# Layer 0's masks added on TensorE for two sequences, and the late tiles' plan played in steps

## The chip, the cores and the metric

The kernel runs on one core of a Trainium2 chip. The metric is device time in microseconds (us) of one launch, as a median over runs.

## The reference

Four sequences of 256 tokens, 256 features wide (1024 tokens), pass through two layers. Each of the four blocks is preceded by a layer norm and followed by a residual addition.

1. Layer 0, attention: 16 heads of 16, q and k with rms-norm over 256 features and rope, a causal window of 128 keys:

```python
mask = (q_idx >= k_idx) & (q_idx - k_idx <= WINDOW - 1)      # WINDOW = 128
scores = jnp.einsum('bhqd,bhkd->bhqk', q, k) * scale
scores = jnp.where(mask[None, None], scores, -jnp.inf)
probs = jax.nn.softmax(scores, axis=-1)
```

2. Layer 0, feed-forward: 256 to 1024 to 256 with relu, weights stored as 4-bit integers with scales per block of 64, plus low-rank (rank 16) additions.
3. Layer 1, scan: `dt = softplus(...)`, `h[t] = exp(dt A) h[t-1] + dt B x` for 16 states per feature, `y = sum_n h C`.
4. Layer 1, a transformer block of its own: causal attention with 32 heads of 128 over 4 key heads, then a mixture of 32 experts (sigmoid router plus bias, 8 experts per token, their weights normalised) and a shared expert:

```python
_, idx = jax.lax.top_k(router_scores + expert_bias[None, :], TOPK)   # TOPK = 8
w = jnp.take_along_axis(router_scores, idx, axis=1)
w = w / jnp.sum(w, axis=-1, keepdims=True)
moe = jnp.einsum('tei,te,eih->th', act, wfull, Wd)                    # act = silu(g) * u
```

## The kernel before

**Streams and order.** The program is written as Python generators ("streams"). `timed(stream, (lo, hi, n), ...)` gives the parts of a stream (from one `yield` to the next) marks that run from `lo` to `hi`; `play` always continues the stream whose next mark is smallest, until those that must finish have done so. What is issued in that order lands on the queue of its engine in that order[...]. (SP only starts DMAs; scatters, DMAs with indices, are started by POOL.) PSUM is cut into banks of 128x512 f32: six of tag "w", which `ps(...)` hands out in turn, and two of tag "acc".

**Layer 0's attention**, `l0_attention(b)` for sequence b, has two tiles of 128 queries.
- `l0_project` makes q and k, normalised and rotated, in `qpads[t]` and `kpads[t]`: 32 columns per head, of which 16 are the features. `turn_heads` (L345, L346) transposes them, so that four heads lie at rows 0, 32, 64 and 96 of `qT` and `kT`. q carries a negative scale, so scores are negative of the usual ones, and the lowest stands for the largest.
- `l0_lowest`, once for each of eight pairs of heads, computes the scores of a head: queries of the first tile against 128 keys, queries of the second against 256, two matmuls with 16 rows each, into one bank `l0_sc` (L360). Then DVE runs two `tensor_tensor_reduce` per head (L367), each of which adds a mask (0 or a large number) and takes the minimum over the keys. The minimum goes to column 16 of the head in `qpads[t]`. In the profile each of them is a CUSTOM_DVE operation and a DVE_READ_ACCUMULATOR.
- `qpads` are then transposed anew (L345). With the constant −1 in column 16 of `kpads`, the 17-row products of `l0_softmax` (L381) give scores with the minimum taken off; ACT takes the exponential (L388), and POOL zeroes what the window excludes (L393, L397).
- `l0_values` (L409) multiplies by the values, `l0_divide` (L418 to L422) divides by the sum, `l0_close` (L430, L434) applies the output weights and adds to the residual x.

Sequence 0's attention is played together with the dequantisation of the feed-forward weights (L238, L241, L245, L250, with their low-rank products `lora_up` L240 and `lora_dn` L249) and the start of sequence 1. Sequence 1's `l0_lowest` then comes between parts of sequence 0's softmax, values, close and feed-forward (`feed_forward`, L460 to L503). Sequences 2 and 3 do layer 0 later, beside scans (L506 to L590) and layer 1's attention (L603 to L737) of earlier sequences.

**The experts.** `route(b)` computes the router for a sequence and, by prefix counts (`rank`), the place of every token and expert among the slots of that expert (`mo_at`, L909). POOL scatters the tokens' rows to these slots in DRAM: 16 scatters `slots<-mo_row,mo_at` a sequence (L918). Experts work on tiles of 128 slots; this input has 73 tiles with work. `plan(nm, n, early)` computes which expert each tile has and where its rows lie: an early plan, after the third sequence, for the first EARLY = 16 tiles, which are full already, and a late plan, after the last, for the others (LATE = 80 places). A plan is a chain of some 30 small DVE operations with two PE products in it: `late_pc` counts tokens per expert, `late_pv` (L831) spreads the result to all partitions. Out of `plan` come `regs` (first row and expert, loaded into registers), `which`, `lo`, `hi` and `arm`.

`experts` is pipelined over steps: load of a tile's rows (`slots_in`, L1215, on SP), transpose `flip` (L1225), gate and up products (`gate`, L1233), expert weight and destination `mx_wj`, `at` (`weigh`, L1248 to L1255), activation (L1263), transpose (L1268), down product (L1278), copy `mx_o` (L1286) and a scatter with addition to one of four sums in DRAM (L1287, on POOL). The first FEWEST = 64 steps are fixed; a Switch on the number of tiles chooses how many follow. At the end the four sums are read back and added to x (L1366, L1371).

The last route, the shared expert, the first 64 expert steps and the late plan are played together:

```python
def planned():
    yield
    tables.append(plan("late", LATE, False))
    yield
...
streams = [
    timed(shared(), (-1, 3, 2), (10, 18, 4)),
    timed(experts(FEWEST, range(FEWEST), under_way), (-2, FEWEST - 2, FEWEST)),
    timed(planned(), (6, 6, 2)),
]
play([timed(last_route[0], (0, 3, 3), (3, 5, 9))], streams)
```

Of the kernel before, what the change touches and what calls it, by code (L numbers as in the profile page):

```python
# [8 lines left out]
F32 = mybir.dt.float32  # L9
I32 = mybir.dt.int32  # L10
BF16 = mybir.dt.bfloat16
AF = mybir.ActivationFunctionType
ALU = mybir.AluOpType
AX = mybir.AxisListType
SYNC = mybir.DependencyInfo(mybir.DependencyClass.Sync, mybir.DependencyReason.DATA)

P = 128
# [8 lines left out]
NH0 = 16  # L26
HD0 = 16
# [16 lines left out]
EARLY = ((B - 1) * S * TOPK - NE * (P - 1)) // P  # L44
# [8 lines left out]
def block_kernel(ctx: ExitStack, tc, out, a):  # L53
    nc = tc.nc
    V, A, G, T = nc.vector, nc.scalar, nc.gpsimd, nc.tensor
# [3 lines left out]
    const = ctx.enter_context(tc.tile_pool(name="const", bufs=1, side="left"))  # L59
# [6 lines left out]
    def ps(name, tag="w"):  # L66

        return psum.tile([P, 512], F32, tag=tag, name=name, bufs=6 if tag == "w" else 2)
# [23 lines left out]
    early = ExitStack()  # L92
# [7 lines left out]
    ident = const.tile([P, P], F32, tag="ident", name="ident")  # L100
# [4 lines left out]
    masks = const.tile([P, 4 * P], F32, tag="masks", name="masks")  # L105
# [8 lines left out]
        pattern=[[1, P]], compare_op=ALU.is_gt, fill=BIG, base=0, channel_multiplier=-1,  # L114
    )
    mask_first = masks[:, P : 2 * P]
    mask_window = masks[:, 2 * P : 4 * P]
    mask_causal = masks[:, 0 : 2 * P]


    ones16 = const.tile([P, P], BF16, tag="ones16", name="ones16")
# [132 lines left out]
    l0 = early.enter_context(tc.tile_pool(name="l0", bufs=1, side="right"))  # L254
# [94 lines left out]
    def l0_pair(u):  # L349
        return [(2 * u + i, 32 * ((2 * u + i) % 4)) for i in range(2)], u // 2  # L350

    def l0_lowest(b, u, seq):

        pair, j = l0_pair(u)
        qT, kT = seq["qT"], seq["kT"]
        scs = [ps(f"l0_sc{b}_{h}") for h, _ in pair]
        for q, cols in ((0, slice(0, P)), (1, slice(P, 3 * P))):
            for (h, r0), sc in zip(pair, scs):
                rows_ = slice(r0, r0 + HD0)
                T.matmul(  # L360
                    sc[:, cols], qT[rows_, j, q * P : (q + 1) * P],
                    kT[rows_, j, 0 : cols.stop - cols.start], start=True, stop=True,
                )
        for (h, _), sc in zip(pair, scs):
            junk = l0.tile([P, 3 * P], F32, tag="junk", name=f"l0_junk{b}_{h}", bufs=1)
            for t, cols, mask in ((0, slice(0, P), mask_first), (1, slice(P, 3 * P), mask_window)):
                V.tensor_tensor_reduce(  # L367
                    junk[:, cols], sc[:, cols], mask, 1.0, 3.0e38,
                    ALU.add, ALU.min, seq["pads"][t][:, h, HD0 : HD0 + 1],
                )  # L370

    def l0_softmax(b, u, seq):

# [62 lines left out]
    def l0_attention(b):  # L436


        seq = {}
        yield from l0_project(b, seq)  # L440
        for u in range(NH0 // 2):
            l0_lowest(b, u, seq)
            yield
        for t in range(2):
            turn_heads(
                seq["qT"][:, :, t * P : (t + 1) * P], seq["pads"][t], f"l0_ptr{b}_{t}_2",
                V.tensor_copy if t == 0 else A.copy,
            )
        prs = {}
        for u in range(NH0 // 2 + 2):  # L450
            if u < NH0 // 2:
                prs[u] = l0_softmax(b, u, seq)
            if u >= 2:
                i = u - 2
                if i % 4 == 0:
                    seq["av"] = halves(ps(f"l0_av{b}_{i // 4}", "acc"))
                l0_values(b, i, seq, prs.pop(i))
                if i % 4 == 3:
                    l0_divide(b, i // 4, seq)
            yield  # L460
        l0_close(b, seq)
# [312 lines left out]
    def plan(nm, n, early):  # L774

        def small(name, n=NE, dtype=F32):
            return end[0].tile([P, n], dtype, tag=f"plan_{name}", name=f"{nm}_{name}", bufs=1)

        c16 = stat.tile([P, NE], BF16, tag="mo_chosen16", name=f"{nm}_c16", bufs=1)
        V.tensor_copy(c16, chosen)
        pc = ps(f"{nm}_pc")[:, 0:NE]

        T.matmul(pc, ones16, c16, start=True, stop=True)
        count, tiles, cum, junk = small("count"), small("tiles"), small("cum"), small("junk")
        ti = small("ti", dtype=I32)
        ex, one = small("ex", 1), small("one")
        total = small("total", 1)
        j, used, vals = small("j", 1), small("used", 1), small("vals", 3)  # L790
        V.tensor_copy(count, pc)
        V.tensor_scalar(ti, count, 0.0 if early else float(P - 1), None, ALU.add)
        V.tensor_scalar(ti, ti, 7, None, ALU.arith_shift_right)
        V.tensor_copy(tiles, ti)
        if not early:
            V.tensor_tensor(tiles, tiles, taken, ALU.subtract)
        V.tensor_tensor_scan(cum, ones_ne, tiles, 0.0, ALU.mult, ALU.add)
        V.tensor_copy(total, cum[:, NE - 1 :])
        V.tensor_scalar(junk, cum, part, None, ALU.is_le)
        V.tensor_reduce(ex, junk, AX.X, ALU.add)  # L800
        V.tensor_scalar(one, enum, ex, None, ALU.is_equal)
        V.tensor_tensor(cum, cum, tiles, ALU.subtract)
        if early:

            V.tensor_scalar(taken, cum, -1.0, float(EARLY), ALU.mult, ALU.add)
            V.tensor_scalar(taken, taken, 0.0, None, ALU.max)
            V.tensor_tensor(taken, taken, tiles, ALU.min)
        else:
            V.tensor_tensor(cum, cum, taken, ALU.subtract)

        V.tensor_tensor(junk, one, cum, ALU.mult)
        V.tensor_reduce(j, junk, AX.X, ALU.add)
        V.tensor_tensor(j, part, j, ALU.subtract)
        V.tensor_scalar(j, j, float(P), None, ALU.mult)
        if early:
            V.tensor_copy(vals[:, 1:2], ex)
            V.scalar_tensor_tensor(vals[:, 0:1], ex, float(CAP), j, ALU.mult, ALU.add)
        else:
            live = small("live", 1)
            V.tensor_tensor(junk, one, count, ALU.mult)  # L820
            V.tensor_reduce(used, junk, AX.X, ALU.add)
            V.tensor_scalar(live, ex, float(NE) - 0.5, None, ALU.is_lt)
            V.tensor_tensor(vals[:, 1:2], ex, live, ALU.mult)
            V.tensor_tensor(vals[:, 2:3], used, j, ALU.subtract)
            V.scalar_tensor_tensor(j, ex, float(CAP), j, ALU.mult, ALU.add)
            V.tensor_tensor(vals[:, 0:1], j, live, ALU.mult)

        rows_of = 2 if early else 3
        pv = ps(f"{nm}_pv")[:, 0 : rows_of * n].rearrange("p (q i) -> p q i", q=rows_of)
        for q in range(rows_of):  # L830
            T.matmul(  # L831
                pv[:, q, :], vals[:, q : q + 1].to_broadcast([P, P]), ident[:, 0:n],
                start=True, stop=True,
            )
        which = end[0].tile([P, n], F32, tag=f"{nm}_which", name=f"{nm}_which", bufs=1)
        V.tensor_copy(which, pv[:, 1, :])
        regs = end[0].tile([1, 2, n], I32, tag=f"{nm}_regs", name=f"{nm}_regs", bufs=1)
        V.tensor_copy(regs[:, 0, :], pv[0:1, 0, :])
        V.tensor_scalar(regs[:, 1, :], pv[0:1, 1, :], 2.0 * P, None, ALU.mult)
        if early:  # L840
            return regs, which, None, None, None

        arm = end[0].tile([1, 1], I32, tag="arm", name="arm", bufs=1)
        V.tensor_scalar(arm, total[0:1], float(EARLY - FEWEST), None, ALU.add)

        lo = end[0].tile([P, n], F32, tag="lo", name="lo", bufs=1)
        hi = end[0].tile([P, n], F32, tag="hi", name="hi", bufs=1)
        spare = small("spare", 1)
        V.tensor_scalar(spare, part, float(CAP), None, ALU.add)
        V.tensor_scalar(lo, pv[:, 2, :], part, spare, ALU.is_le, ALU.mult)  # L850
        V.tensor_scalar(hi, lo, float(CAP - 1), None, ALU.max)
        return regs, which, lo, hi, arm

    taken = stat.tile([P, NE], F32, tag="taken", name="taken", bufs=1)

    LATE = -(-(TILES - EARLY) // 4) * 4
# [3 lines left out]
    def route(b, row):  # L860
# [51 lines left out]
            )  # L912

        if b == B - 2:
            tables.append(plan("early", EARLY, True))
        for t in range(2):
            for k in range(TOPK):
                inst = G.indirect_dma_start(  # L918
# [58 lines left out]
    def timed(stream, *pieces):  # L977


        marks = [lo + (hi - lo) * i / n for lo, hi, n in pieces for i in range(n)]  # L980
        return [stream, marks, 0, False]
# [346 lines left out]
            yield  # L1328


    def planned():
        yield
        tables.append(plan("late", LATE, False))
        yield

    under_way = ahead, {}, {}, {}, {}, {}, {}, {}
    streams = [
        timed(shared(), (-1, 3, 2), (10, 18, 4)),
        timed(experts(FEWEST, range(FEWEST), under_way), (-2, FEWEST - 2, FEWEST)),
        timed(planned(), (6, 6, 2)),  # L1340
    ]
    play([timed(last_route[0], (0, 3, 3), (3, 5, 9))], streams)
    with tc.manual_schedule():
# [137 lines left out]
```

## Time and profile before

| | us |
|---|---|
| time before, median of 3 runs | 1109.64 |
| lowest and highest of these | 1108.83, 1111.13 |
| profiled execution, its own time | 1098.13 |
| profiled execution, span of its trace | 1096.4 |

| engine | busy, us | share of the span | instructions |
|---|---|---|---|
| PE (matmul) | 932.8 | 85% | 4589 |
| DVE | 727.3 | 66% | 2237 |
| POOL | 510.1 | 47% | 534 |
| ACT | 491.1 | 45% | 1503 |

The stages, by the start of their instructions in the trace of the profiled execution: sequence 0's projections to 32 us, its scores to 57.7, softmax, values and close to 106.3, its feed-forward to 138.0, its scan to 223.7, layer 1's attention for all sequences from there to 902, the last route to 914.4, the remaining scatters to 1074.6, and the final sums to the end.

Times in a trace are counted in us from the start of the span. PE is TensorE's matmul row and PEld its weight loads; DVE is VectorE, ACT ScalarE, POOL GpSimd. "L360" is line 360 of the kernel. The granted clock is the share of full speed at which TensorE ran; over the whole span it is 0.908 in the mean. A line of a timeline gives start, duration, engine, line, operation, output and inputs, count, and in brackets the idle time before it and what ended that. A line of a group gives count, busy time and mean duration in ns, and idle time before it.

### The profile page before, as it was taken

What the parts mean: (1) busy time and instruction counts of PE and PEld (TensorE: products, weight loads), DVE (VectorE), ACT (ScalarE), POOL (GpSimd) and SP (SyncE); (2) the same over time, 40 slices, a digit from 0 to 9 for tenths busy, and PEclk for the clock granted to TensorE, in tenths of its full rate; (3) what the DMA queues carried; (4) which work ended last, traced back from release to release, by engine and by line L of the source; (5) the groups of instructions that cost most, each with busy time, mean ns of one, the idle gap of its engine ahead of it and who ended that gap; (6) DMA issues with size and microseconds to landing.
All of it is one profiled execution on the core that took longest, in us unless ns stands there. A gap on an engine that the chain in (4) does not pass through costs nothing. (4 is left out here: it accounts for less than half of the span.)

```text
span 1096.4 us, 15761 instructions
## 1 busy us (share of the span) xinstructions
PE 932.8 (85%) x4589; PEld 696.5 (64%) x4589; DVE 727.3 (66%) x2237; ACT 491.1 (45%) x1503; POOL 510.1 (47%) x534
## 2 busy tenths in 40 slices
PE   4898976478898999999899989899998997999770
PEld 2655743355666687767677766677877875777650
DVE  6746149947996775899686489896475536555454
ACT  2031233324655364656555466655564554444330
POOL 5030123413456332344865135775335624888781
PEclk9576776788898999999999989999999998999995
DMA  8985999960110111111222473223223327799867
GB/s 214 236 180 132 255 246 241 245 217 26 39 49 30 39 39 38 49 49 49 62 80 71 134 226 101 72 99 101 68 83 99 108 84 252 147 155 150 155 73 206
DMA packets 131716, 134.31 MB, mean 123 GB/s; under 512 B 10592, under 2 KB 125440, under 8 KB 131616
## 3 DMA queue, kind: packets, MB, share of 16 engines
q1 hardware_dynamic: 118032, 114.12, 39.0%
q0 software_dynamic: 13584, 19.05, 9.6%
q8 instruction: 40, 0.66, 0.3%
q14 instruction: 60, 0.49, 0.1%
HBM read 70.45 MB, written 62.69 MB: 121 GB/s over the span
## 5 line engine op out<-in xcount | busy, mean ns | idle before, releaser
L607 POOL TENSOR_TENSOR at_q_rot<-at_q_t,at_q_t 128x512 f32<-128x512 f32 x64 | 85.0, 1328 | 139.6 <-DVE at_q_t L603 116.8
L686 ACT ACTIVATE at_pr<-at_pr,at_low 128x128 f32<-128x128 f32 (+1 forms) x256 | 113.6, 445 | 52.0 <-DVE at_low L682 49.7
L737 PE MATMUL at_po<-at_wo,at_oT 128*128 128x256 f32 x512 | 129.6, 387 | 2.2 <-ACT at_oT L730 2.1
L655 PE MATMUL at_pq<-at_hT,at_wq 128*128 128x256 f32 x512 | 125.7, 389 | 3.1 <-DVE at_q_t L603 1.8
L696 POOL TENSOR_SCALAR at_pr<-at_pr,at_rden 128x128 f32<-128x128 f32 x128 | 87.8, 695 | 80.4 <-DVE at_rden L691 62.9
L1287 POOL DMA_INDIRECT sum<-mx_o,at x73 | 113.8, 1559 | 24.1 <-issue 9.4
L581 POOL TENSOR_TENSOR sm_y<-sm_y,sm_hc 128x512 f32<-128x512 f32 x60 | 77.2, 1287 | 86.0 <-DVE sm_hc L579 82.9
L655 PEld LDWEIGHTS at_pq<-at_hT,at_wq 128*128 128x128 f32 x512 | 98.0, 196 | 19.7 <-DVE at_q_t L603 2.0
L737 PEld LDWEIGHTS at_po<-at_wo,at_oT 128*128 128x128 f32 x512 | 95.4, 193 | 17.3 <-ACT at_oT L730 3.4
L603 DVE TENSOR_TENSOR at_q_t<-at_pq,rope 64x512 f32<-64x512 f32 x128 | 88.1, 688 | 15.4 <-POOL at_k_rot L607 12.9
L568 ACT ACTIVATE decay<-sm_dt,na 128x255 f32<-128x255 f32 x128 | 58.7, 500 | 64.4 <-DVE sm_h L574 58.4
L574 DVE TENSOR_TENSOR_SCAN sm_h<-decay,sm_w 128x512 f32<-128x512 f32 x64 | 84.5, 1320 | 1.3
L719 ACT COPY at_pT<-at_pa 128x512 f32<-128x512 f32 x64 | 37.2, 581 | 104.1 <-PE at_pa L712 104.0
L918 POOL DMA_INDIRECT slots<-mo_row,mo_at x64 | 64.4, 1007 | 39.0 <-DVE mo_at L909 21.1
L682 DVE CUSTOM_DVE_ANT_0 at_pr<-at_sc,masks 128x128 f32<-128x128 f32 (+1 forms) x256 | 78.4, 353 | 4.6 <-PE at_sc L678 3.0
L678 PE MATMUL at_sc<-at_k_rot,at_q_rot 128*128 128x256 f32 x256 | 76.5, 380 | 0.0
L727 PE MATMUL at_pav<-at_pT,at_v 128*128 128x512 f32 x128 | 67.4, 609 | 2.8 <-DVE sm_hc L579 1.3
L601 DVE TENSOR_TENSOR at_q_t<-at_pq,rope 128x512 f32<-128x512 f32 x64 | 43.8, 684 | 38.4 <-PE at_pq L655 38.0
L393 POOL TENSOR_SCALAR_AFFINE_SELECT l_pr<-l_pr 128x512 f32<-128x512 f32 x32 | 22.4, 700 | 97.7 <-ACT l_pr L388 97.7
L700 ACT ACTIVATE at_pr<-at_pr,at_rden 128x256 f32<-128x256 f32 x128 | 57.9, 501 | 8.2 <-DVE at_rden L691 8.0
L677 PEld LDWEIGHTS at_sc<-at_k_rot,at_q_rot 128*128 128x128 f32 x256 | 47.9, 190 | 12.7 <-issue 2.7
L1233 PE MATMUL bank<-wgu,mx_xT 128*128 x192 | 52.0, 394 | 3.9 <-DVE mx_act L1263 3.4
(357 smaller groups left out, 2038.9 us busy)
## 6 DMA issues: line engine op xcount, KB each, us to landing
slots<-zero SPq DMA_DIRECT2D x32, 1156.0 KB, 20.3
at_wq<-in_Wq_dram SPq DMA_DIRECT2D x64, 256.0 KB, 2.7
at_wo<-in_Wo_dram SPq DMA_DIRECT2D x64, 256.0 KB, 2.8
xg<-slots SPq DMA_DIRECT2D x73, 144.5 KB, 3.1
sum<-zero SPq DMA_DIRECT2D x4, 1152.0 KB, 12.7
wgu<-in_Wg_dram SPq DMA_DIRECT2D x32, 128.0 KB, 3.0
wgu<-in_Wu_dram SPq DMA_DIRECT2D x32, 128.0 KB, 3.3
wd<-in_Wd_dram SPq DMA_DIRECT2D x8, 512.0 KB, 6.7
```

Of the source, the lines that this page charges most:

```text
L574: V.tensor_tensor_scan(hs.rearrange("p c l -> p (c l)"), da.rearrange("p c l -> p (c l)"), w.rearrange("p c l -> p (c l)"), 0.0, ALU.mult, ...
L581: G.tensor_tensor(y, y, hc, ALU.add)
L603: V.tensor_tensor(t2[lo : lo + 64], src[hi : hi + 64], sin[hi : hi + 64].unsqueeze(1).to_broadcast([64, n, S]), ALU.mult,)
L607: G.tensor_tensor(dst, t1, t2, ALU.add)
L655: T.matmul(pq[:, i, :], wq[:, c, i * HD : (i + 1) * HD], hT[:, c, :], start=c == 0, stop=c == 1,)
L678: T.matmul(sc[:, P : 3 * P], qT[:, i, P:S], kT[:, 0, :], start=True, stop=True)
L682: V.tensor_tensor_reduce(pr[:, cols], sc[:, cols], mask, 1.0, 3.0e38, ALU.add, ALU.min, low[:, k : k + 1],)
L686: A.activation(pr[:, cols], pr[:, cols], AF.Exp, scale=-1.0, bias=low[:, k : k + 1], accum_out=den[:, k : k + 1],)
L696: scaled.append(G.tensor_scalar(prs[i][:, cols], prs[i][:, cols], rden[:, k : k + 1], None, ALU.mult).ins)
L727: T.matmul(pav, v_sb[:, 0, cols], pT[0], start=True, stop=False)
L737: T.matmul(po[:, t, :], oT[:, i, t * P : (t + 1) * P], wo[:, i, :], start=h0 + i == 0 and t == 0, stop=h0 + i == NH - 1 and t == 1, skip_g ...
L1287: G.indirect_dma_start(out=sums[i % SUMS], out_offset=bass.IndirectOffsetOnAxis(ap=at, axis=0), in_=o, in_offset=None, compute_op=ALU.add,)
```

## The change

There are two parts.

First, in sequences 0 and 1 the masks reach the scores on TensorE. A bf16 identity and a bf16 copy of the three 128x128 mask blocks are made once. For each head a matmul of the two (128x128 by 128x384) starts the bank, and the two score matmuls accumulate onto it. One `tensor_reduce` per head then takes the three minima of 128 keys into a small tile `low`; once per sequence, `l0_lowered` brings them into column 16 of `qpads`: a copy for the first query tile, and the smaller of two for the second. Sequences 2 and 3 keep the former code as `l0_lowest_late`.

Second, `plan` becomes a generator that yields between its operations. The early plan is still run through at once. The late plan is a stream of its own with marks from 5 to 13 in 11 parts, in place of a single part at mark 6.

```diff
+    ident16 = const.tile([P, P], BF16, tag="ident16", name="ident16")
+    masks16 = const.tile([P, 3 * P], BF16, tag="masks16", name="masks16")
+    V.tensor_copy(ident16, ident)
+    V.tensor_copy(masks16, masks[:, P:])
...
     def l0_lowest(b, u, seq):
 
+        pair, j = l0_pair(u)
+        qT, kT = seq["qT"], seq["kT"]
+        scs = [ps(f"l0_sc{b}_{h}") for h, _ in pair]
+        for sc in scs:
+            T.matmul(
+                sc[:, 0 : 3 * P], ident16, masks16, start=True, stop=False, skip_group_check=True
+            )
+        for q, cols in ((0, slice(0, P)), (1, slice(P, 3 * P))):
+            for (h, r0), sc in zip(pair, scs):
+                rows_ = slice(r0, r0 + HD0)
+                T.matmul(
+                    sc[:, cols], qT[rows_, j, q * P : (q + 1) * P],
+                    kT[rows_, j, 0 : cols.stop - cols.start],
+                    start=False, stop=True, skip_group_check=True,
+                )
+        for (h, _), sc in zip(pair, scs):
+            V.tensor_reduce(
+                seq["low"][:, h, :], sc[:, 0 : 3 * P].rearrange("p (c k) -> p c k", c=3),
+                AX.X, ALU.min,
+            )
+
+    def l0_lowest_late(b, u, seq):
+
         pair, j = l0_pair(u)
...
+    def l0_lowered(seq):
+
+        low = seq["low"]
+        at = slice(HD0, HD0 + 1)
+        V.tensor_copy(seq["pads"][0][:, :, at], low[:, :, 0:1])
+        V.tensor_tensor(seq["pads"][1][:, :, at], low[:, :, 1:2], low[:, :, 2:3], ALU.min)
...
         yield from l0_project(b, seq)
+        seq["low"] = l0.tile([P, NH0, 3], F32, tag="low", name=f"l0_low{b}", bufs=2)
         for u in range(NH0 // 2):
-            l0_lowest(b, u, seq)
+            (l0_lowest if b < 2 else l0_lowest_late)(b, u, seq)
             yield
+        if b < 2:
+            l0_lowered(seq)
...
         T.matmul(pc, ones16, c16, start=True, stop=True)
+        yield
         count, tiles, cum, junk = small("count"), small("tiles"), small("cum"), small("junk")
...
-        return regs, which, lo, hi, arm
+        tables.append((regs, which, lo, hi, arm))
...
         if b == B - 2:
-            tables.append(plan("early", EARLY, True))
+            for _ in plan("early", EARLY, True):
+                pass
...
-    def planned():
-        yield
-        tables.append(plan("late", LATE, False))
-        yield
-
...
-        timed(planned(), (6, 6, 2)),
+        timed(plan("late", LATE, False), (5, 13, 11)),
```

The diff shows one of ten such `yield`s in `plan`. The order of instructions per engine, before and after, differs as follows. POOL's and SP's orders are the same. PE gets 32 loads of `ident16` and 32 mask matmuls; one `lora_up` product goes behind the first pair of scores; `late_pc` comes earlier, and `late_pv` some four expert steps later. On DVE, the four instructions per head (32 heads) become one, and four small ones are new; sequence 0's last two reductions come ahead of a `w_dn` addition that they stood behind; the late plan's operations lie between those of the expert steps; `late_c` goes ahead of the last route's `mo_at`, and `late_count` stands between its two `mo_at` operations.

More of the change, by code (lines that the diff above doesn't have):

```diff
@@ L116, in block_kernel @@
     mask_first = masks[:, P : 2 * P]
-    mask_window = masks[:, 2 * P : 4 * P]
     mask_causal = masks[:, 0 : 2 * P]
+    ident16 = const.tile([P, P], BF16, tag="ident16", name="ident16")
+    masks16 = const.tile([P, 3 * P], BF16, tag="masks16", name="masks16")
+    V.tensor_copy(ident16, ident)
+    V.tensor_copy(masks16, masks[:, P:])
     ones16 = const.tile([P, P], BF16, tag="ones16", name="ones16")
@@ L365, in l0_lowest @@
             junk = l0.tile([P, 3 * P], F32, tag="junk", name=f"l0_junk{b}_{h}", bufs=1)
-            for t, cols, mask in ((0, slice(0, P), mask_first), (1, slice(P, 3 * P), mask_window)):
+            for t, cols, mask in ((0, slice(0, P), mask_first), (1, slice(P, 3 * P), masks[:, 2 * P :])):
                 V.tensor_tensor_reduce(
@@ L796, in plan @@
             V.tensor_tensor(tiles, tiles, taken, ALU.subtract)
+        yield
         V.tensor_tensor_scan(cum, ones_ne, tiles, 0.0, ALU.mult, ALU.add)
         V.tensor_copy(total, cum[:, NE - 1 :])
+        yield
         V.tensor_scalar(junk, cum, part, None, ALU.is_le)
@@ L801, in plan @@
         V.tensor_scalar(one, enum, ex, None, ALU.is_equal)
+        yield
         V.tensor_tensor(cum, cum, tiles, ALU.subtract)
@@ L809, in plan @@
             V.tensor_tensor(cum, cum, taken, ALU.subtract)
+        yield
         V.tensor_tensor(junk, one, cum, ALU.mult)
@@ L814, in plan @@
         V.tensor_scalar(j, j, float(P), None, ALU.mult)
+        yield
         if early:
@@ L826, in plan @@
             V.tensor_tensor(vals[:, 0:1], j, live, ALU.mult)
+        yield
         rows_of = 2 if early else 3
@@ L834, in plan @@
             )
+        yield
         which = end[0].tile([P, n], F32, tag=f"{nm}_which", name=f"{nm}_which", bufs=1)
@@ L840, in plan @@
         if early:
-            return regs, which, None, None, None
+            tables.append((regs, which, None, None, None))
+            return
+        yield
         arm = end[0].tile([1, 1], I32, tag="arm", name="arm", bufs=1)
         V.tensor_scalar(arm, total[0:1], float(EARLY - FEWEST), None, ALU.add)
+        yield
         lo = end[0].tile([P, n], F32, tag="lo", name="lo", bufs=1)
```

## The prediction

> **What bounds the kernel now.** I read the slices of the page first, then a table of windows cut at the stage borders, then the chain, and last the timelines of the places that the change touches.
>
> ```profile
> PE   4898976478898999999899989899998997999770
> DVE  6746149947996775899686489896475536555454
> PEclk9576776788898999999999989999999998999995
> ```
>
> One slice is 27.4 us. PE is the full row nearly everywhere, and its clock is low only in the first eleven slices, where layer 0 runs. The windows (us, then busy time and count per engine, granted clock, DMA share, GB/s) give each stage its limit:
>
> ```profile
> 31.00:50.30 19.30, 18.01 (x79) 13.03 (x78) 14.97 (x60) 0.58 (x1) 0.00 (x0) 0.50 0.91 230
> 57.70:82.00 24.30, 23.56 (x130) 14.53 (x130) 9.32 (x25) 10.23 (x30) 8.73 (x16) 0.78 0.78 174
> 82.00:106.30 24.30, 22.68 (x111) 13.85 (x110) 15.47 (x53) 2.70 (x6) 2.51 (x4) 0.65 0.42 118
> 106.30:124.00 17.70, 14.07 (x43) 9.76 (x44) 5.76 (x28) 2.67 (x7) 1.26 (x1) 0.61 1.10 245
> 165.70:223.70 58.00, 27.11 (x97) 17.89 (x95) 54.37 (x73) 16.58 (x40) 22.36 (x18) 0.68 1.09 246
> 245.00:902.00 657.00, 611.82 (x3113) 469.38 (x3112) 478.16 (x1427) 363.20 (x1113) 318.73 (x344) 0.98 0.25 75
> 934.70:1074.60 139.90, 115.61 (x595) 92.18 (x592) 70.43 (x332) 52.44 (x195) 113.81 (x73) 0.95 0.82 133
> ```
>
> Sequence 0's scores (31 to 50) are PE-bound, 18.01 of 19.30 us, at half clock all the way; DVE is close behind. 82 to 106 is PE again, with sequence 1's scores between sequence 0's value products. Then sequence 0's feed-forward, its scan (DVE, 54.4 of 58 us), and from 245 layer 1's attention on PE. Each stage starts with the result of the one before, and the order within an engine is fixed at build time, so what sequence 0's chain loses in layer 0 shifts all that follows. The tail is another matter:
>
> ```profile
> DMA 7%; PE 3%; issue 2%; DVE 1%; POOL 1%; SPq 0%; ACT 0%; POOLq 0%; DVEq 0%
> 914.37 1.03 POOL L918 DMA_INDIRECT slots<-mo_row,mo_at  x1 [21.09 <-DVE mo_at L909]
> 934.70 1.62 POOL L1287 DMA_INDIRECT sum<-mx_o,at  x1 [0.31 <-DVE at L1253]
> ```
>
> The page's chain covers only the last seventh. POOL's timeline says more: from 914.37 it issues 16 scatters of slots at 1.265 us each, then at once 73 scatters of sums at 1.86 us, with no gap over 0.3 us except 1.8 us about the Switch. What starts POOL at 914.37 is mo_at of the last route; from there POOL sets the end.
>
> **The late plan in steps.** Before, its instructions stand as one block on DVE (914.7 to 922.7) and PE waits 4.66 us for late_vals ahead of late_pv (919.85). All lies under POOL's scatters. The first mx_o is ready at 928.75, 6 us before POOL reaches its scatter at 934.70, so the wait removed is worth 0. It issues no DMA; SP's loads of expert numbers and rows, POOL's queue and their order stay the same. What moves: late_c goes ahead of the route's mo_at; late_count, which waits for PE's late_pc, now stands between the two mo_at operations, with the second and its scatters behind it. The first is not behind it. POOL needs the second eight scatters later, 10 us, and late_pc waits at most one expert's products (some 2 us). If that cover were gone it would cost those 2 us. late_pv comes four expert steps later, and its values are first needed for steps from EARLY on: the 16 slots and 16 sum scatters, some 50 us, cover it. Between −0.3 and +0.3, I take 0.
>
> **DVE in the scores.** Groups by form, 30 to 58 (busy, mean ns of one | idle before):
>
> ```profile
> L360 PE MATMUL l_sc<-l_kT,l_qT 16*128 16x256 f32 x32 | 11.6, 643 | 0.0
> L360 PE MATMUL l_sc<-l_kT,l_qT 16*128 16x128 f32 x32 | 9.4, 486 | 1.3 <-DVE qpad L367 1.3
> L367 DVE CUSTOM_DVE_ANT_0 l_junk<-l_sc,masks 128x256 f32<-128x256 f32 x16 | 6.7, 420 | 0.0
> L367 DVE CUSTOM_DVE_ANT_0 l_junk<-l_sc,masks 128x128 f32<-128x128 f32 x16 | 4.6, 287 | 3.3 <-PE l_sc L360 2.2 <-DVE qpad L367 0.6
> L367 DVE DVE_READ_ACCUMULATOR2_ANT qpad<- 128x1 f32 x32 | 2.7, 84 | 0.0
> ```
>
> A head now takes two custom operations and two reads, 0.56 us from start to start (41.07 to 41.63 in DVE's timeline). One TENSOR_REDUCE over 384 columns replaces them. No row has that form; the custom pair gives 0.13 us more per 128 columns, so 0.42 + 0.13 = 0.55 us long, some 0.48 of pitch: a gain of 0.1 × 16 = 1.3 to 1.6 us a sequence. At the floor it is the 256-column custom's 0.34 of pitch (gain 3.5), at the ceiling 0.65 (loss 1.5). Since PE ends last, the gain counts only where PE waits on DVE for a bank. The two conversions to bf16 lie at 4 to 11 us, where DVE waits for loads and for POOL: 0, and 0.3 us each if that cover were gone. The two small operations of l0_lowered cost some 0.2 us each, and stand between the last reduction and the transposes; they are in the gain above. The change issues no DMA; SP's zero fills, which wait for sequence 0's dequantisation buffers (62.6 to 95), shift with that sequence and are done by 232, long before the first sum scatter.
>
> **The masks on PE.** 32 products 128x384 in bf16, each with the load of ident16. The nearest row is sel, at half clock and 256 columns, six in a row:
>
> ```profile
> 159.11 1.46 PE L561 MATMUL sm_pbc<-sm_bc,sel 96*128 96x256 bf16 x6
> 88.78 1.65 PE L360 MATMUL l_sc<-l_kT,l_qT 16*128 16x128 f32 x8
> 90.36 1.50 PE L409 MATMUL l_av<-l_pr,l_v 128*32 128x256 f32 x8
> 91.78 1.65 PE L360 MATMUL l_sc<-l_kT,l_qT 16*128 16x128 f32 x8
> 42.51 2.06 PE L360 MATMUL l_sc<-l_kT,l_qT 16*128 16x128 f32 x14
> ```
>
> Successive starts are 0.21 us apart, so 384 columns are 0.32 us at half clock and 0.16 at full. The Trainium skill ("TensorE: Matmul & The Clock Gate", Part 1) says that the clock is full after one busy window of about 3.4 us. The row 31.00:50.30 speaks against that: PE shows 18.01 of 19.30 us busy at 0.50. In this trace the clock rises only after 128-row products nearly fill such a stretch (L290 and L292 from 59.3: full at 64.8). By the rule the stage would be at full clock and a mask cost 0.16 (16 × 0.16 = 2.6); by the trace 0.32 (5.1). I take the trace.
>
> Second, the masks stand between pairs. Scores of 16 rows for different heads run beside each other: 14 matmuls start inside 42.51 to 44.1, some 0.55 us per head with neighbours following on, against 1.58 us per pair (0.79 per head) where other work stands around it, as at 88.78. The skill's "TensorEngine Tiling (Array Packing)", Key Properties, says a change of tiling mode drains TensorE, which speaks against this change: by it every pair becomes an isolated one, 8 × 0.48 = 3.8 us more. The trace shows several pairs already apart, by lora products or waits (16 matmuls take 4.34 us from 45.95). I take 1.5 and keep 0 and 3.8.
>
> Sequence 0: masks 16 × 0.32 = +5.1, overlap +1.5, waits of PE on DVE that a shorter DVE takes up −2.5 (1.3 in the groups' PE row; the loads' row has 2.5), and −0.9 at the end, where its last two reductions no longer stand behind w_dn (54.12, itself waiting 2.12 us for lora_dn). Sum +3.2. Its softmax, 57.72, starts near 61.
>
> Sequence 1: its pairs lie on sequence 0's path in 82 to 119. Twelve heads at half clock, four at full: 12 × 0.32 + 4 × 0.16 = +4.5. Overlap +0.8 (pairs at 82 to 84 only; those after are isolated already). Off that −1.7, for one clock window of 3.4 us that the masks' 128-row work keeps at full near 82. Sum +3.6.
>
> Total +6.8 on the span of 1096.4. The profiled execution itself took 1098.13, 11.5 under the median of 1109.64; the shift is the same to either, so 1109.6 + 6.8 = 1116.4.
>
> **Rivals.**
> 1. The clock stays up (faster). The masks are full-array work: 0.64 us of a 3.4 us window per pair. At 85.3 the clock falls and at 102.4 it rises. If it holds at 1.0 there, three pairs with their values shrink from 3 × 3.07 to 3 × (0.80 + 0.75 + 0.32) us, −3.6, and 97.5 to 102 by 2.2. With masks of pairs at full clock (+1.3), sequence 0's +3.2, and one window won before the rise at 122.9 (ff_pu from 113.5), −3.4, the sum is −4.7: 1104.9. It decides on one window, 82 to 85.3, now filled by scores that leave most of the array empty. For it: 75 to 82 is at full clock on similar mixed work. Against: 85 to 95 contains 128-row value products half the time and stays at 0.50. 0.25.
> 2. One of the two stretches only, or DVE's cover is larger than I read (11.1 of 12.3 us busy in 38 to 50): PE's additions go partly into waits. 0 ± 2: 1109.6. 0.17.
> 3. The steps don't do what they say: the Switch's number comes late, so POOL starves at step 16. Place: 950 or so; price: one plan's 8 us. Needs late_pv later by over 30 us. 0.03, time 1124.
>
> **How the numbers follow.** A measurement of this kernel can tell about 0.2% (2.2 us) from no change. The forecast (1112.5 to 1121) has 0.55, rival 1 0.25, rival 2 0.17, rival 3 0.03. Faster 0.25; same 0.15 (rival 2 but its edges); slower 0.60. The range 1105 to 1121 leaves out the better half of rival 1 and rival 3 with the worst overlap; the forecast's own range is 1112.5 to 1121.
>
> **What would show it.** Right: a mask group 128x384 near 0.32 us pitch in sequence 0; softmax of sequence 0 (57.72) at 60 to 62; x add L434 (106.27) at 112 to 114; the first slots scatter (914.37) near 921, and the same 160 us from it to the last sum scatter. Wrong: the clock at 0.78 or more in 82 to 106, or the shift at L434 below 3 us; or a gap in POOL's row after 914, which would make the plan the cause.

## The result: 0.5% slower, and the profile after

The changed kernel takes 1113.66 us in the median of 20 runs (1102.18 to 1116.01), the kernel before 1107.36 in 20 (1103.61 to 1111.13). The ratio is 1.0049 with an interval of 1.0033 to 1.0065: 5.4 us slower by the ratio, 6.3 by the medians. The prediction had +6.8.

Its profiled execution took 1109.11 us with a span of 1107.4; that of before had 1098.13 and 1096.4, less than the shortest of the 20 runs of before here (1103.61). The two spans differ by 11.0 us, more than the medians, so the pair must be read stage by stage. The slices of the page after:

```profile
PE   4999876378899999999999988899989995999770
DVE  6644249947995865899686489885575533655453
PEclk9585876788898999999999989999999996999895
```

The windows of the changed kernel, cut at the same borders (us, then busy time and count per engine, granted clock, DMA share, GB/s):

```profile
31.30:52.60 21.30, 21.30 (x91) 9.51 (x88) 14.70 (x27) 0.58 (x1) 0.00 (x0) 0.50 0.90 233
58.30:79.30 21.00, 20.29 (x128) 12.85 (x128) 9.59 (x25) 10.21 (x30) 8.10 (x15) 0.88 0.81 185
79.30:111.50 32.20, 31.50 (x124) 17.61 (x124) 13.83 (x16) 2.70 (x6) 2.58 (x6) 0.58 0.51 134
916.50:940.40 23.90, 10.22 (x40) 7.84 (x39) 6.96 (x44) 3.94 (x15) 15.41 (x16) 0.65 0.55 205
940.40:1081.20 140.80, 121.72 (x629) 99.85 (x627) 75.11 (x356) 53.91 (x201) 112.25 (x72) 0.95 0.82 132
```

In the first, PE is now busy for all of it, still at half clock. The second is shorter than before (21.0 against 23.5 us, at 0.88 instead of 0.78), the third longer (32.2 us, at 0.58; before, the same work went from 81.2 to 106.3). Then the tail: 24.0 us where the kernel before had 20.3, and 140.8 where it had 136.0. The groups of the score stage, 30 to 62:

```profile
L370 PE MATMUL l_sc<-l_kT,l_qT 16*128 16x256 f32 x32 | 8.5, 629 | 0.0
L376 DVE TENSOR_REDUCE l_low<-l_sc 128x3 f32<-128x384 f32 x16 | 8.3, 553 | 6.5 <-PE l_sc L370 6.5
L364 PE MATMUL l_sc<-masks,ident 128*128 128x384 bf16 x16 | 6.6, 515 | 0.0
L370 PE MATMUL l_sc<-l_kT,l_qT 16*128 16x128 f32 x32 | 6.4, 497 | 0.0
```

DVE now waits 6.5 us for PE's scores. The reduction takes 0.553 us, as estimated (0.55). Laid side by side, the two traces have these stages (us, from the first start named to the second):

```
                                                   before    after
first score -> softmax of sequence 0                25.69    26.97
softmax -> first denominator (l_den)                23.48    21.02
first denominator -> residual addition (x, l_po)    25.06    32.23
residual addition -> scan's first step              60.18    57.06
scan's first step -> attention of layer 1           71.18    71.17
attention of layer 1 -> first of the last slots    676.74   676.71
first of the last slots -> first sum scatter        20.33    23.98
first -> last sum scatter                          136.02   140.78
```

Only 2.8 us of the 11.0 are in front of layer 1's attention, and 8.4 in the tail, where the prediction had put 0. (The first score, or mask, itself starts 0.7 us earlier, so attention starts 2.1 us later.) So there were two theories, and a third on the clock:

- A: the prediction. The masks are paid on PE's path in both sequences; the plan costs nothing, and the tail of this one trace has another cause.
- B: the plan in steps lets POOL starve in the tail, and the masks cost little.
- C: what changes is mostly where the stretches at half clock fall.

The comparisons below were made on three chips, where the kernel before took 1098.82, 1100.23 and 1106.04 us; each ratio is to the kernel before on the same chip.

### The profile page after: what moved, and what is told of

Read it like the earlier page. It is cut to its first block, busy times and chain, and to the rows that moved or that the text cites. A ratio compares the mean times of both kernels' runs of the same rounds, so it can differ in the third digit from the quotient of the medians.

```text
span 1107.4 us, 15719 instructions
## 1 busy us (share of the span) xinstructions
PE 941.0 (85%) x4621; PEld 696.8 (63%) x4621; DVE 724.6 (65%) x2147; ACT 490.6 (44%) x1503; POOL 509.3 (46%) x534
## 4 chain that ended last, share of the span: by engine, by line
PE 49%; DVE 26%; POOL 6%; issue 5%; DMA 5%; ACT 5%; another core or an unknown queue 1%; SPq 1%; POOLq 0%; DVEq 0%; ACTq 0%
PE at_po L776 5%; PE at_pq L694 5%; DVE sm_h L613 4%; DVE at_q_t L642 4%; PE bank L1284 3%; PE at_pav L766 3%; PE ff_pu L521 3%; DMA sum<-mx_o,at 2%; PE l_sc L370 2%; PE l_sT L417 2%; DVE sm_hc L618 2%; PE at_sc L717 2%; DVE sm_w L611 2%; DVE at_pr L721 2%; PE ff_pd L536 2%
```

## The experiments

**Parts of the change, one at a time.** The plan in steps alone (former scores everywhere), the masks alone (plan as one block), and the masks in one sequence only:

```diff
-            (l0_lowest if b < 2 else l0_lowest_late)(b, u, seq)
+            l0_lowest_late(b, u, seq)                            # plan only
...
-        timed(plan("late", LATE, False), (5, 13, 11)),
+        timed(planned(), (6, 6, 2)),                             # masks only
...
-            (l0_lowest if b < 2 else l0_lowest_late)(b, u, seq)
+            (l0_lowest if b == 0 else l0_lowest_late)(b, u, seq) # one sequence; b == 1 likewise
```

> The late plan in steps, with the former scores in all four sequences. Theory A (the prediction): the plan is hidden under POOL's scatters, 0 +- 1 us against the kernel before, and 20.3 us from the first of the last 16 slots scatters to the first sum scatter. Theory B (the tail): the stall of the changed kernel's trace there (23.9 us, then five gaps in POOL's row, 10.5 - 2.1 = 8.4 us in all) comes from the plan's steps lying between the expert steps; then +5 to +9 us here, with gaps in POOL's row after the first sum scatter.

> Masks on TensorE in sequences 0 and 1, with the late plan as one block as before. Theory A: +5 to +8 us, all of it there when sequence 0's residual addition after the attention starts. Theory B: +1 to +3 us, since the changed kernel's trace shows layer 1's attention only 2.1 us later. Theory C (the clock's windows): the front's shift depends on how the half-clock stretches fall, between -2 and +6, and the 12 first layer-0 windows tell.

> Masks on TensorE in sequence 0 alone, plan as one block. Theory A: +3.2 (2 to 5), softmax of sequence 0 starts near 61. From the changed kernel's trace (58.29 against 57.72, the scores starting 0.7 earlier) it is rather +0.6 to +1.3 at that point; then the rest is the clock's.

> Masks on TensorE in sequence 1 alone, plan as one block. Theory A: +3.6 (2 to 6), seen between 81 and the residual addition of sequence 0. Theory C: sequence 0's output products (12 of l_po) fall in a half-clock window, 5.35 instead of 2.86 us, as in the changed kernel; +5 there, partly given back by 140.

Measured: plan only 1.0014 (0.9996 to 1.0032), masks only 1.0023 (1.0004 to 1.0041), masks in sequence 0 0.9996 (0.9979 to 1.0013), in sequence 1 1.0015 (0.9993 to 1.0038). Only masks-only is clear of 1, by a little; the traces say more. First score to softmax is 25.67 in plan-only and 25.31 in sequence-1-only, but 26.98 in masks-only and in sequence-0-only: masks in sequence 0 cost 1.3 to 1.7 us there. First denominator to residual addition is 28.17 and 28.23 where sequence 1 has no masks, 32.23 and 32.36 where it has: 4.1 us, with the output products l_po at half clock in all four. The clock alone moves this stretch nearly as much: with the former scores in sequence 1 it takes 25.06 us in the profile of before and 25.07 to 28.23 in four others. So of the 7.2 us between the first two profiles, some 3 are theory C's. From the first of the last slots scatters to the first sum scatter all four take 20.31 to 20.36, plan-only as well.

Where the 4.1 us of sequence 1 are is seen in PE's timeline, the first lines of plan-only, the next of masks-only, both at half clock:

```profile
86.71 1.50 PE L442 MATMUL l_av<-l_pr,l_v 128*32 128x256 f32 x8
88.13 1.65 PE L386 MATMUL l_sc<-l_kT,l_qT 16*128 16x128 f32 x8
89.72 1.50 PE L442 MATMUL l_av<-l_pr,l_v 128*32 128x256 f32 x8
...
98.34 2.18 PE L386 MATMUL l_sc<-l_kT,l_qT 16*128 16x128 f32 x8
100.45 5.49 PE L463 MATMUL l_po<-wo,l_oT 128*128 128x256 f32 x12
```

```profile
89.49 1.50 PE L445 MATMUL l_av<-l_pr,l_v 128*32 128x256 f32 x8
90.92 0.82 PE L364 MATMUL l_sc<-masks,ident 128*128 128x384 bf16 x2
91.67 1.65 PE L370 MATMUL l_sc<-l_kT,l_qT 16*128 16x128 f32 x8
93.25 1.50 PE L445 MATMUL l_av<-l_pr,l_v 128*32 128x256 f32 x8
...
102.38 0.53 PE L364 MATMUL l_sc<-masks,ident 128*128 128x384 bf16 x1
102.83 1.64 PE L370 MATMUL l_sc<-l_kT,l_qT 16*128 16x128 f32 x4
104.41 0.50 PE L364 MATMUL l_sc<-masks,ident 128*128 128x384 bf16 x1
104.84 1.65 PE L370 MATMUL l_sc<-l_kT,l_qT 16*128 16x128 f32 x4
106.42 5.48 PE L466 MATMUL l_po<-wo,l_oT 128*128 128x256 f32 x12
```

A pair with its values takes 3.76 us in place of 3.01: 0.75 for two masks. The last pair before l_po takes 4.04 instead of 2.11: there one head's mask stands between the two heads' scores, and the second head no longer runs beside the first.

**The changed kernel again.**

> The changed kernel once more, beside the kernel before on this chip, and with a second profile of it. If the wait of 8.4 us in the tail of its first profile belongs to the kernel (theory B), the second has it too, near 24 us from the first of the last slots scatters to the first sum scatter. If it was one execution's (theory A), 20.3 us as in the four kernels so far, and the time is the sum of masks and plan alone, +2 to +6.

Measured: 1.0039 (1.0016 to 1.0062), and 20.32 us from the first of the last slots scatters to the first sum scatter. POOL's timeline, first the changed kernel's first profile, then this one:

```profile
916.46 1.04 POOL L969 DMA_INDIRECT slots<-mo_row,mo_at  x1 [21.09 <-DVE late_count L831]
940.45 1.62 POOL L1338 DMA_INDIRECT sum<-mx_o,at  x1 [3.97 <-DVE at L1304]
943.48 1.59 POOL L1338 DMA_INDIRECT sum<-mx_o,at  x1 [1.41 <-DVE at L1304]
```

```profile
919.81 1.04 POOL L969 DMA_INDIRECT slots<-mo_row,mo_at  x1 [22.77 <-DVE late_count L831]
940.13 1.62 POOL L1338 DMA_INDIRECT sum<-mx_o,at  x1 [0.31 <-issue]
942.06 1.59 POOL L1338 DMA_INDIRECT sum<-mx_o,at  x1 [0.30 <-issue]
```

The wait of 3.97 us and those after it are gone, with the same program. Theory B falls for this part. The wait also came in a kernel that has the plan as one block (four masks together with DVE's former form, below), on the third chip:

```profile
915.20 1.04 POOL L969 DMA_INDIRECT slots<-mo_row,mo_at  x1 [21.09 <-DVE mo_at L959]
939.82 1.62 POOL L1338 DMA_INDIRECT sum<-mx_o,at  x1 [4.56 <-DVE at L1304]
942.32 1.59 POOL L1338 DMA_INDIRECT sum<-mx_o,at  x1 [0.88 <-DVE at L1304]
```

All four kernels profiled on that chip took 22.7 to 24.6 us there, three of them with the plan in one block; all eight on the other two chips took 20.3. The rest of the tail goes with it: from the first to the last sum scatter 139.6 to 141.3 us there, 135.9 to 138.4 on the other two. So the 8.4 us of the first pair of profiles belong to where they were taken, not to the change. In the changed kernel's first profile DVE waits 12.51 us for pd, a product that PE had ended by 927.3, and PE then 10.29 us for DVE; what holds DVE up stays open.

**PE's cost and DVE's gain apart.** The mask products added to the kernel before, with DVE's work kept; and one reduction per head on DVE, with no masks:

```diff
+        if b < 2:
+            for sc in scs:
+                T.matmul(sc[:, 0 : 3 * P], ident16, masks16, start=True, stop=True)
         for q, cols in ((0, slice(0, P)), (1, slice(P, 3 * P))):   # DVE as before
...
-        for sc in scs:
-            T.matmul(
-                sc[:, 0 : 3 * P], ident16, masks16, start=True, stop=False, skip_group_check=True
-            )                                                     # no masks, one reduction
```

> The kernel before with the mask products of sequences 0 and 1 added on TensorE, overwritten by the scores, and VectorE's work as before: the cost on PE alone. By the prediction's terms, from the first score to sequence 0's softmax 25.67 + 5.1 + 1.5 = 32.3 us. If the gain on VectorE was only small (26.97 with both), 27 to 28. In sequence 1 (softmax to residual addition) as with both, 53 to 54.

> No masks in the minima of sequences 0 and 1: scores as before on PE, one TENSOR_REDUCE per head on DVE. The minimum is then over masked keys as well, which leaves the softmax the same in exact arithmetic. VectorE's gain alone. By the prediction's terms, from the first score to the softmax 25.67 - 2.5 - 0.9 = 22.3 us; in sequence 1 nothing (49.4 from softmax to residual addition). If PE alone sets the stage, 25.4.

Measured: 1.0016 (0.9980 to 1.0051) and 0.9945 (0.9916 to 0.9975), the second 6.1 us less. Sequence 0, all of it at half clock, from the first score (or mask) to the softmax, in us; in brackets, to the next product after the scores, and from there:

| | no masks on PE | masks between pairs |
|---|---|---|
| DVE's former form | 25.69 (18.18 + 7.50), before | 28.87 (22.11 + 6.75) |
| one reduction per head | 19.51 (13.82 + 5.69) | 26.97 (21.28 + 5.69), changed |

```profile
45.95 4.34 PE L360 MATMUL l_sc<-l_kT,l_qT 16*128 16x128 f32 x16
57.72 0.80 PE L381 MATMUL l_sT<-l_qT,l_kT 17*128 17x256 f32 x2 [0.68 <-ACT l_qT L346]
31.96 0.85 PE L384 MATMUL l_sc<-masks,ident 128*128 128x384 bf16 x2
60.83 1.43 PE L416 MATMUL l_sT<-l_qT,l_kT 17*128 17x256 f32 x6 [0.68 <-ACT l_qT L351]
```

(The first two lines are of the kernel before, the others of the extra masks.) The two halves do not add up: the masks cost 3.2 us with DVE's former form and 7.5 with the new one, and the new form gains 6.2 us without masks and 1.9 with them. The 32.3 us that the prediction's terms gave for the extra masks did not come. There PE's busy time rises by 5.15 us (22.37 to 27.52), as 16 masks at 0.32 would have it, but its idle time falls by 2.0 us, 1.3 of it waits for DVE's reductions: part of the masks goes into PE's waits. In sequence 1 (softmax to residual addition) the extra masks gave 50.01, below the 53 to 54 expected; there the clock was back at full from 106.4, before the twelve l_po products, which then took 2.86 us instead of 5.48. The scores in the run without masks, windows and timeline:

```profile
31.80:45.60 13.80, 13.15 (x74) 10.43 (x73) 11.64 (x23) 0.59 (x1) 0.00 (x0) 0.50 0.73 209
```

```profile
43.07 2.58 PE L366 MATMUL l_sc<-l_kT,l_qT 16*128 16x128 f32 x16
45.58 1.11 PE L195 MATMUL l_pT<-ident,l_xn 128*128 128x128 f32 x4
48.63 1.97 PE L350 MATMUL l_ptr<-ident,qpad 128*128 128x128 f32 x8
51.27 1.65 PE L413 MATMUL l_sT<-l_qT,l_kT 17*128 17x256 f32 x8 [0.67 <-ACT l_qT L351]
```

The last four heads' scores take 2.5 us; in the kernel before the same sixteen matmuls, at the same clock, take 4.3 (45.95). There DVE is busy for 11.1 of the 12.3 us from 38 to 50.3, and banks come free one by one behind it: PE's waits are hidden in the length of its groups (over the whole stage PE shows 22.37 us busy before and 18.19 here, with the same products). From the last score to the softmax it is 5.7 us instead of 7.5, for the last transposes no longer wait for reductions that stand behind w_dn.

**Masks of four heads together**, in sequence 0 alone:

```diff
+        if u % 2 == 0:
+            seq["scs"] = [ps(f"l0_sc{b}_{2 * u + i}") for i in range(4)]
+            for sc in seq["scs"]:
+                T.matmul(sc[:, 0 : 3 * P], ident16, masks16, start=True, ...)
+        scs = seq["scs"][2 * (u % 2) : 2 * (u % 2) + 2]
```

> Masks in sequence 0 alone, with the mask products of four heads together ahead of the eight scores of two pairs, so that two pairs may overlap again. If the masks between pairs cost overlap (1.5 us in the prediction), from the first score to the softmax 26.98 becomes 25.5 to 26.2; if they cost none, 27.0 or, with four banks taken at once, some tenths more.

Measured: 0.9972 (0.9944 to 1.0000), first score to softmax 23.70 us: 3.3 less than with a mask pair between each two pairs of scores, and 2.0 less than before. Its timeline:

```profile
41.73 1.46 PE L365 MATMUL l_sc<-masks,ident 128*128 128x384 bf16 x4
43.12 1.68 PE L373 MATMUL l_sc<-l_kT,l_qT 16*128 16x128 f32 x16
```

Four masks in 1.39 us, then four heads in 1.44 before the next product starts (44.56). In the changed kernel two heads alone take 1.59:

```profile
48.68 1.65 PE L370 MATMUL l_sc<-l_kT,l_qT 16*128 16x128 f32 x8
50.27 0.82 PE L364 MATMUL l_sc<-masks,ident 128*128 128x384 bf16 x2
```

Four masks stand together only for the last eight heads, which give 2.1 of the 3.3 us; the first eight have their masks in groups of two, two, three and one.

Four masks together, but DVE's former form:

> The fourth corner: sequence 0 with the mask products of four heads together on PE, overwritten by the scores, and DVE's former pair of operations per head. If the price of masks between pairs is lost overlap on PE alone, 28.87 - 3.28 = 25.6 us from the first score to the softmax. If DVE's former 0.56 us a head with its waits sets a floor, no lower than the 25.67 of the kernel before, and rather 26 to 27.

Measured: 29.26 us, ratio 1.0022 (1.0003 to 1.0041). Neither expectation came true: in the kernel as built the four masks do not stand together, presumably since with DVE's longer form the banks come free later, and single masks stand between scores (at 38.60, 40.17, 44.97, 46.55). So this run does not isolate what it was meant to.

**Four together in both sequences**, with the plan in steps:

> The changed kernel, plan in steps included, with the mask products of four heads together in both sequences. Sequence 0: 23.7 us, 3.3 less than the changed kernel. Sequence 1, where value products stand between the pairs: no gain from overlap, 0 to 1 us. In all 3 to 4 us under the changed kernel, so 0.9995 to 1.0015 of the kernel before.

Measured: 1.0018 (0.9997 to 1.0040), just above the 0.9995 to 1.0015 that was expected. Sequence 0 takes 23.69 us, first denominator to residual addition 32.09: as expected, no gain in sequence 1, where other work stands between the pairs anyway.

**Every mask twice**, for its own price and for the rival of the clock:

> Every mask product of sequences 0 and 1 twice (the second overwrites the first), plan as one block: the price of a mask product by itself, and a trial of the rival that its full-array work raises the clock. At half clock 16 x 0.32 to 0.375 us = +5.1 to +6.0 in sequence 0 (26.98 to 32.1 to 33.0) and about +4.5 in sequence 1. If the added work brings the clock up, sequence 0 takes less than 30 us and shows windows at 1.0 before 57.

Measured: 1.0012 (0.9986 to 1.0037), and 29.06 us in sequence 0. At half clock successive masks start 0.32 us apart, as expected, but the sum of +5.1 to +6.0 did not come, for the clock did rise, twice:

```profile
32.10:35.50 3.40, 3.40 (x24) 1.73 (x22) 2.54 (x5) 0.00 (x0) 0.00 (x0) 1.00 0.29 56
35.50:60.10 24.60, 23.94 (x97) 11.96 (x94) 14.40 (x28) 1.21 (x3) 0.00 (x0) 0.50 1.04 263
97.00:110.00 13.00, 10.67 (x62) 6.48 (x60) 8.41 (x13) 0.96 (x2) 0.00 (x0) 1.00 0.80 228
```

The first of these is one window of 3.4 us, in which work is done that takes 6.8 at half clock: 16 × 0.32 − 3.4 = 1.7, against 2.1 measured. That window follows one (28.7 to 32.1) in which PE has 128-row products from 29.30 on, and only the last microsecond of them are masks; so where the window's border fell had a part in it. The third line covers l_po, which the masks-only run passes at 0.50:

```profile
97.00:111.80 14.80, 14.80 (x41) 9.20 (x39) 5.95 (x6) 0.37 (x1) 0.00 (x0) 0.50 1.04 268
```

With twice the masks, first denominator to residual addition took 26.33 us, against 32.23 with one mask: more work on PE, and 5.9 us less. That is rival 1 as the prediction described it, at twice the density. It is one profile, and the place of the windows alone moved this stretch by 3.2 us above; but in all ten runs the mean granted clock was 0.906 to 0.920, against 0.894 to 0.907 for the kernel before on the same chip.

**No masks in all four sequences**, since the run without them was the fastest:

> As the run without masks, in all four sequences: one TENSOR_REDUCE per head on DVE, no mask anywhere in the minima (the same softmax in exact arithmetic). From the first score to sequence 0's softmax 19.5 us, as there. If DVE's time matters in sequences 2 and 3 too, which stand beside layer 1's attention on PE, faster than that run's 0.9945, near 0.993; if PE alone bounds that stretch, the same 0.9945.

Measured: 0.9995 (0.9981 to 1.0010). Neither came true: the gain is lost. The front is the same (19.51 us), but from attention to the last slots it is 684.68 us instead of 676.91. Most of the difference is there by the end of sequence 3's scores; the run without masks in two sequences, then this one, from about the same place in the work:

```profile
463.40:470.20 6.80, 6.80 (x38) 5.50 (x38) 6.80 (x27) 3.70 (x13) 3.82 (x5) 1.00 0.19 58
```

```profile
463.90:470.70 6.80, 6.80 (x22) 4.95 (x19) 5.13 (x12) 2.96 (x10) 4.01 (x4) 0.50 0.01 2
```

For two windows of 3.4 us the clock is at half, in which 22 matmuls run instead of 38. Counted from the first output product of layer 1's attention, this kernel's 81st is 0.6 us earlier than the other's, its 129th 6.1 us later. Two windows at half clock can account for 3.4 us of that; the rest is not explained. Why the clock fell is open as well. In the window before, both kernels have the same two groups of scores with the same wait of 0.46 us between them (from 461.30 and from 461.45), but the window's border lies some 0.65 us later against that work here. Its place is as good an explanation as the shorter reduction, and no run separates the two. Nor is a long stretch special to this kernel: with the former scores in sequences 2 and 3 it takes 676.1 to 677.1 us in eight profiles and 680.1 to 681.7 in five, and the changed kernel has one of each (676.71 and 681.61).

## Why the prediction came out right, and where its terms were wrong

- The sign was right, and the size: +6.8 against +5.4 by the ratio (+6.3 by the medians), and +4.3 for the changed kernel's second comparison (1.0039; +2.2 by the medians). That they are so near owes something to luck: the measured times leave a microsecond or two open, masks-only came to no more than +2.5 us (0.4 to 4.5), and the terms were off as follows.
- Sequence 0: predicted +3.2, measured +1.3. To the last score it lost 3.1 us (18.18 to 21.28), where masks, overlap and DVE's waits had been put at +5.1 +1.5 −2.5 = +4.1; behind the scores it gained 1.8 (7.50 to 5.69), where 0.9 had been put. What failed was the adding of terms as if each were independent of the others. Alone, the masks cost 3.2 us with DVE's former form, not 6.6, since PE had waits to put them into, as rival 2 had it in part; alone, the shorter DVE form gained 6.2, not 3.4, since PE's waits for banks also stand in its longer groups, like the 4.34 us for sixteen, and not only in the groups' waits, where they had been read. Together, with PE busy without a gap (21.30 of 21.30 us), DVE's form is worth only 1.9. Lost overlap was sized at 1.5; grouping the masks brings back 3.3, near the 3.8 that was kept as the upper end.
- The price of a mask was right: 0.32 us between successive masks at half clock, 0.35 in a group of four, 0.38 with the change to and from scores. In this trace too the clock did not follow from PE being busy (21.30 of 21.30 us at 0.50), against the rule in the Trainium skill's "TensorE: Matmul & The Clock Gate", Part 1. The skill's "TensorEngine Tiling (Array Packing)", Key Properties, has TensorE drain at a change of tiling mode; the 3.3 us are in line with that, though the runs do not tell a drain from the order alone.
- Sequence 1: predicted +3.6, measured +4.1 between first denominator and residual addition, by profiles alike in clock. The −1.7 for one window kept at full clock did not come in that stretch. A term that was not in the sum did: some 1.2 us for the two heads whose scores stand one after the other (4.04 against 2.11 us, less 0.75 for two masks).
- The plan: predicted 0. The traces agree (20.31 us, and 20.32 in the changed kernel), but 1.0014 (−0.4 to +3.5 us) doesn't exclude a microsecond or two. The first of the last scatters does wait for late_count by the profile, yet it starts 0.85 us after mo_tops, as before (0.86).
- Rival 1 did not happen with one mask per head: 71.7 us of the first 130 are at half clock in both profiles. With two per head the clock was higher.
- The places named beforehand were less exact than the total: softmax at 58.29 (60 to 62 named), residual addition at 111.53 (112 to 114), first slots scatter at 916.46 (near 921). POOL's row did have gaps after 914, named as a sign against the plan; they came from elsewhere. Two readings were wrong: from the first of the last slots scatters to the last sum scatter it was 156.4 us before, not 160, and the gaps about the Switch are 1.61 and 0.84 us.

Parts and whole add up loosely: plan 1.0014 and masks 1.0023 make 1.0037, against 1.0049 and 1.0039.

The version that beats both is the one without masks in the minima of sequences 0 and 1: 0.9945 of the kernel before, and beside the changed kernel on the same chip 0.9945 / 1.0039 = 0.991.

## What to carry to other kernels

When work moves from a near-bound engine to the bound one, measure the two halves apart, and in both orders: here −6.2 and then +7.5 us, or +3.2 and then −1.9, hid behind a net of +1.3. Dropping the part that cost (softmax needs any shift, not the exact minimum) kept the gain in two sequences; in all four it was lost. Small-row matmuls that overlap across heads lose that overlap to full-array products between them, so put such products together (3.3 us here). A tail that looks worse in one trace may belong to the chip; profile the same program twice before blaming the edit.

## What was not expected of the hardware

Time follows the clock. Over the 20 runs of the changed kernel the mean granted clock goes from 0.893 to 0.908 and the time from 1116.0 to 1102.2, with a correlation of −0.93 and a slope of 9 us per 0.01. The half-clock stretches are whole windows of 3.4 us (in the profile of before five from 85.3 to 102.4, four from 109.2 to 122.9) whose place against the work differs from run to run, so a kernel with this much of layer 0 at the edge moves by several microseconds with no change to it: the same front, from the first score to layer 1's attention, took 205.6 us in the profile of before and 201.4 in that of plan-only, whose front is the same program. More PE work went with a shorter stage once (26.33 against 32.23 us, every mask twice), and less DVE work with a longer one (684.68 against 676.91, no masks in all four sequences); the cause of the second is not shown.
